# The normalised activations in DRAM by row and channel instead of by channel and row

## The chip, the cores and the metric

The kernel runs on one core of a Trainium2 chip. The core has a matrix engine (TensorE, PE in the profile), three engines for elementwise work (VectorE = DVE, ScalarE = ACT, GpSimd = POOL), a queue engine (SyncE = SP), and 16 DMA engines that move data between DRAM and the on-chip memory of 128 partitions. The metric is the device time of one execution in microseconds. The kernel before takes 7,697.9 us (median of 3, from 7,692.57 to 7,713.86).

## What is computed

The input x has the shape [16, 16, 256, 256] (batch, channel, row, column), in fp32. Two layers follow each other, each with a group norm ahead of it and a residual sum after it:

```python
x = x + L0(_gn(x))       # Fourier layer: FFT, products with poles and residues, back
x = x + L1(_gn(x))       # the layer that the change concerns
```

With the norm's result z in place of x, layer 1 is, cut to its core:

```python
xs = z.reshape(B * C, 1, H, W)
f = mish(conv2d(xs, W1, b1))                    # conv1: 1 -> 4 features, 3x3
top, bot = f[:, :, :H2], f[:, :, H2:]           # upper and lower half of the rows
ker = conv2d(relu(conv2d(bot, Wred, bred)), Wspan, bspan)
top_inv = (patches3x3(top) * ker[:, None]).sum(axis=2)          # involution
shuffled = concatenate([top_inv, roll(bot, -1, axis=1)], 3)     # channels regrouped
out = mish(conv2d(shuffled, W2, b2))            # conv2: 64 -> 16 channels, 3x3
gate = sigmoid(weighted sum of neighbouring channels' means of out)
return z * gate
```

## The kernel before

Four stages run one after the other: `layer0_forward`, `layer0_mix`, `layer0_back` and `layer1`. The tensor zn in DRAM, [16, 16, 258, 258], joins the last two. It holds the norm's result with a border of zeros, so that a 3x3 window needs no special cases.

`layer0_back` (line 753) goes over 16 batches and four groups of four channels. It computes layer 0's result by matmuls (lines 813 and 816), takes the statistics, and writes the norm's result into one of three tiles `zb` (line 830: one half of the channels on VectorE, the other on GpSimd). Two DMAs (line 839) store the tile, each 128 rows of four channels, 1,032 bytes in one piece.

`layer1` (line 849) works by units. A batch has nine: eight with 30 new rows of eight channels (four row blocks j, two channel halves h), and a tail unit with the last rows of all 16 channels. What a unit does:

- `load_rows` (line 913) brings z for the lower half and for the upper half of the picture, in a pool of four buffers. Partition 32 dx + r holds row r of 32, shifted by dx columns, so that the three column taps of the 3x3 filter lie on partitions. Three DMAs bring 32 rows of eight channels each (line 920), two more bring rows 32 and 33 for all three dx (line 928). The tail takes twelve DMAs of ten rows of four channels (line 934). All are issued by SyncE.
- `conv1` (line 940) multiplies 102 partitions (120 in the tail) with the weights. It works by column parity q: one matmul for the odd columns, one for the even ones, each of four channels by 128 columns, and so reads every second column. An fp32 matmul is two passes in the profile.
- `lower` (line 959) applies Mish to the lower half in one activation per group of four channels. `reduce` makes the involution's kernel from it and stores the lower half into the DRAM tensor cf (line 1067, GpSimd's queue).
- `upper` (line 986) does conv1 for the upper half, with eight activations of 32 partitions per group (line 995). `spread` (line 1002) copies them to the shifted partitions on GpSimd. `involution` (line 1010) is one matmul per feature and group and three VectorE operations, and `store_top` writes cf.

Conv2 runs one batch behind. `conv2_rows` (line 1072) loads 17 row pairs from cf on SyncE's queue, in two buffers, and `conv2` (line 1077) makes 48 passes on quarter tiles per call and an activation with a sum. When a batch is done, `gate` (line 1101) reloads z from zn in four parts (line 1113), multiplies by the gate plus the norm's scale (line 1135) and stores the output (line 1136).

The order on TensorE, ScalarE, VectorE and GpSimd is written by hand in the loop at the end of `layer1`. In each step, unit i+2 is loaded, unit i+1 goes through `lower`, `reduce`, `upper` and `spread`, unit i through `involution`, and a piece of conv2 of the batch before is put between them. SyncE carries out its loads in the order in which they are issued. PSUM has two buffers for conv1, three for the involution and reduce, and one for conv2.

Of the kernel before, what the change touches and what calls it, by code (L numbers as in the profile page):

```python
# [18 lines left out]
C = 16  # L19
# [732 lines left out]
@with_exitstack  # L752
def layer0_back(ctx, tc, d, hd, bd, zn, mr, ed):


    nc = tc.nc
    nb = d["x"].shape[0]
    cp = ctx.enter_context(tc.tile_pool(name="bc", bufs=1))
    iy = load(nc, cp, d["iy"], [P, 2, N], "iy")
    ones = load(nc, cp, d["ones"], [P, P], "ones")  # L760

    e1 = cp.tile([P, C, N], F32, name="e1")
    e2 = cp.tile([P, C, N], F32, name="e2")
    for k in range(0, C, 4):
        for i, t in enumerate((e1, e2)):
            nc.sync.dma_start(out=t[:, k : k + 4], in_=ed[:, i, k : k + 4])

    hp = ctx.enter_context(tc.tile_pool(name="bh", bufs=3))
    fp = ctx.enter_context(tc.tile_pool(name="bf", bufs=3))
    sm = ctx.enter_context(tc.tile_pool(name="bs", bufs=2))  # L770
    psf = ctx.enter_context(tc.tile_pool(name="psf", bufs=2, space=PSUM))
    psy = ctx.enter_context(tc.tile_pool(name="psy", bufs=3, space=PSUM))
    psn = ctx.enter_context(tc.tile_pool(name="psn", bufs=1, space=PSUM))

    zero = cp.tile([P, 4, N + 2], F32, name="zero")
    nc.gpsimd.memset(zero, 0.0)
    planes = zn.rearrange("b (p c) y x -> p (b c) y x", p=1)[0]
    for h in range(2):
        for y in (0, N + 1):
            nc.gpsimd.dma_start(out=planes[P * h : P * h + P, y], in_=zero[:, 0])  # L780
    zbuf = [cp.tile([P, 4, 2, N + 2], F32, name=f"zb{i}") for i in range(3)]
    for t in zbuf:
        for x in (0, N + 1):
            nc.gpsimd.memset(t[:, :, :, x : x + 1], 0.0)

    for b in range(nb):
        r2 = fp.tile([P, P], F32, tag="r2", name="r2")
        nc.sync.dma_start(out=r2, in_=bd[b])
        for k0 in range(0, C, 4):
            h = hp.tile([P, 4, 2, N], F32, tag="h", name="h")  # L790
            nc.sync.dma_start(
                out=h.rearrange("p k v x -> p k (v x)"),
                in_=hd[:, b, k0 : k0 + 4].rearrange("f k v x -> f k (v x)"),
            )
            x = hp.tile([P, 4, 2, N], F32, tag="x", name="x")
            nc.sync.dma_start(
                out=x.rearrange("p k h x -> p (k h) x"),
                in_=d["x"][b, k0 : k0 + 4].rearrange("k (h p) x -> p (k h) x", p=P),
            )
            st = sm.tile([P, 4, 6], F32, tag="st", name="st")  # L800
            for k in range(4):
                if k % 2 == 0:
                    pf = psf.tile([P, 2, N], F32, tag="pf", name="pf")
                    nc.tensor.matmul(
                        pf, lhsT=r2, rhs=e1[:, k0 + k : k0 + k + 2], start=True, stop=True
                    )
                    f = fp.tile([P, 2, N], F32, tag="f", name="f")
                    nc.scalar.copy(f, pf)
                py = psy.tile([P, 2, N], F32, tag="py", name="py")
                for yh in range(2):  # L810
                    ys = slice(P * yh, P * yh + P)
# [12 lines left out]
            g0 = k0 // 2  # L824
            nm, rs = mr[:, b, g0 : g0 + 2, 0], mr[:, b, g0 : g0 + 2, 1]
            for _ in group_norm_scalars(nc, sm, psn, ones, mv, 2, nm, rs):
                pass
            z = zbuf[(4 * b + g0 // 2) % 3]
            for g, eng in ((0, nc.vector), (1, nc.gpsimd)):
                eng.tensor_scalar(  # L830
                    z[:, 2 * g : 2 * g + 2, :, 1 : N + 1],
                    x[:, 2 * g : 2 * g + 2],
                    nm[:, g : g + 1],
                    rs[:, g : g + 1],
                    ALU.add,
                    ALU.mult,
                )
            for h in range(2):
                nc.sync.dma_start(
                    out=zn[b, k0 : k0 + 4, 1 + P * h : 1 + P * h + P].rearrange("k p x -> p k x"),  # L840
                    in_=z[:, :, h],
                )


# [4 lines left out]
def layer1(ctx, tc, d, zn, cf, mr, nb):  # L849
# [62 lines left out]

    def load_rows(b, half, j, h):

        z = zp.tile([P, 8, N], F32, tag="z", name="z")
        if j < 4:
            y = H * half + 30 * j
            src = zn[b, 8 * h : 8 * h + 8]
            for dx in range(3):
                nc.sync.dma_start(  # L920
                    out=z[32 * dx : 32 * dx + 32],
                    in_=src[:, y : y + 32, dx : dx + N].rearrange("c y x -> y c x"),
                )
            for i in range(2):

                row = src[:, y + 32 + i, 0:N]
                win = bass.AP(row.tensor, row.offset, [[1, 3], *row.ap])
                nc.sync.dma_start(out=z[96 + 3 * i : 99 + 3 * i], in_=win)
            return z
        y = H * half + 120  # L930
        for dx in range(3):
            for c in range(4):
                p = 40 * dx + 10 * c
                nc.sync.dma_start(
                    out=z[p : p + 10, :4],
                    in_=zn[b, 4 * c : 4 * c + 4, y : y + 10, dx : dx + N].rearrange("c y x -> y c x"),
                )
        return z

    def conv1(z, half, tail, g):  # L940

        k, w = (120, w1t[half]) if tail else (102, w1[half])
        ps = ps1.tile([P, 2, 4, H], F32, tag="c1", name="c1")
        cols = z[:k, 4 * g : 4 * g + 4].rearrange("k c (x q) -> k q c x", q=2)
        for q in range(2):
            nc.tensor.matmul(ps[:, q], lhsT=w, rhs=cols[:, 1 - q], start=True, stop=True)  # L946
        return ps

    class Unit:

# [8 lines left out]
        def lower(self):  # L959

            self.bot = fp.tile([P, 8, 2, H], F32, tag="bot", name="bot")
            for g, cs in enumerate(self.groups):
                ps = conv1(self.z[0], 1, self.tail, g)
                nc.scalar.activation(
                    self.bot[:, cs].rearrange("p c q x -> p q c x"), ps, AF.Mish, bias=b1[1]
                )

        def reduce(self):

# [16 lines left out]
        def upper(self, g):  # L986
# [6 lines left out]
            for f in range(4):  # L993
                for q in range(2):
                    nc.scalar.activation(  # L995
                        self.feat[64 - 32 * q : 96 - 32 * q, f, self.groups[g], :H],
                        ps[32 * f : 32 * f + 32, q],
                        AF.Mish,
                        bias=b1[0][32 * f : 32 * f + 32],
                    )  # L1000
# [100 lines left out]
    def gate(b, acc):  # L1101
# [4 lines left out]
        dst = d["out"][b].rearrange("c (q y) x -> (c q) y x", q=8)  # L1106

        def part(k):
            o = op.tile([P, 8, N + 2], F32, tag="o", name="o")
            src = zn[b, :, 1 + 8 * k, 0:1]  # L1110
            row = N + 2
            src = bass.AP(src.tensor, src.offset, [[row * row, C], [32 * row, 8], [1, 8 * row]])
            nc.sync.dma_start(out=o.rearrange("p y x -> p (y x)"), in_=src)
            return o[:, :, 1 : N + 1]

        o = part(0)
        yield
# [15 lines left out]
        for k in range(4):  # L1133
            following = part(k + 1) if k < 3 else None
            nc.gpsimd.tensor_scalar(o, o, scale, mean2[:, b : b + 1], ALU.mult, ALU.add)  # L1135
            nc.gpsimd.dma_start(out=dst[:, 8 * k : 8 * k + 8], in_=o)
            o = following
            yield

# [67 lines left out]
def layer1_arrays(W1, b1, Wred, bred, Wspan, bspan, W2, b2, Weca):  # L1207
# [43 lines left out]
    g2 = np.repeat(g1[:C], 8, axis=0)  # L1251
    pm = np.zeros((8, C, 3, C, 8), np.float32)
    for k in range(3):
        for c in range(C):
            if 0 <= c + k - 1 < C:
                pm[:, c + k - 1, k, c, :] = 1.0
    return {
        "w1_0": w1.reshape(102, P),
        "w1_1": w1.transpose(0, 2, 1).reshape(102, P),
# [3 lines left out]
        "dw": dw.reshape(P, P),  # L1263
        "dwt": dwt.reshape(P, P),
        "c2": c2.reshape(P, 2, 3, 32),
        "g2": g2,
# [96 lines left out]
def forward(ctx, tc, d):  # L1363
# [43 lines left out]
```

## Time and profile before

| stage | from, us | to, us | what fills it |
|---|---|---|---|
| layer0_forward, layer0_mix | 0 | about 3,050 | not touched by the change |
| layer0_back | about 3,055 | about 3,902 | first load 3,054.7, last store of zn 3,901.6 |
| layer1 | 3,902.3 | 7,700.4 | first load of z to the end |

Busy time over the whole span of 7,700.4 us: TensorE 7,126.0 us (93%), VectorE 4,921.2 (64%), ScalarE 3,678.6 (48%), GpSimd 2,804.5 (36%). The mean granted TensorE clock is 0.965 of full speed. DMA moved 1,442.20 MB, 875.87 MB read from DRAM and 556.47 MB written to it.

Groups that the change touches, with the mean time of one:

| line, engine | what | count | mean ns |
|---|---|---|---|
| L946 PE | conv1 pass, 102 partitions, 512 columns | 2,048 | 646 |
| L946 PE | conv1 pass in the tail, 120 partitions | 128 | 613 |
| L964 ACT | Mish of the lower half, 1,024 elements | 272 | 1,115 |
| L995 ACT | Mish of the upper half, 32 partitions, 512 elements | 2,176 | 680 |
| L830 DVE, POOL | the norm's result into zb, 1,024 elements | 64 each | 812, 1,752 |
| L1135 POOL | gate times z, 2,048 elements | 64 | 2,055 |

How to read them: the means of matmuls contain the overlap of successive passes, so the distance between the weight loads of two passes tells the real pace. A view by slices shows which stage is busy with what; the chain of waits shows what the end of the program hung on; and the waits show who stood still for whom. Idle time of an engine that isn't on the chain costs nothing.

### The profile page before, as it was taken

Reading aid. Unit: us, or ns where it says so; the run is one execution under the profiler, and the core shown is the slowest. Engines: PE = TensorE matmul, PEld = TensorE weight load, DVE = VectorE, ACT = ScalarE, POOL = GpSimd, SP = SyncE. Lnnn points to the kernel's source line nnn. Section 1 sums busy time; section 2 is a strip of 40 time slices with the busy share of each in tenths; the row PEclk is TensorE's granted clock in tenths of the full one; section 3 lists DMA queues with packets and bytes.
Section 4 is the critical chain, followed back from the end, with each engine's and each line's share of the span. In section 5 each row is a group of like instructions: output and inputs, shape, how many; then the busy total and the mean of one; then the engine's idle time right before and its main releaser. Section 6 shows DMA issues by size and latency. Waiting matters only on the chain. (4 is left out here: it accounts for less than half of the span.)

```text
span 7700.4 us, 147483 instructions
## 1 busy us (share of the span) xinstructions
PE 7126.0 (93%) x58728; PEld 4107.7 (53%) x58728; DVE 4921.2 (64%) x9184; ACT 3678.6 (48%) x5387; POOL 2804.5 (36%) x3616
## 2 busy tenths in 40 slices
PE   7889999688888988999978999999999999999997
PEld 5778888566666766777733333333333333333332
DVE  8999865366666665666656666666666666666662
ACT  2223333355555554111146656666566655656662
POOL 2334444200000000111135545555554555555552
PEclk9999999899999999999989999999999999999998
DMA  3444444333333333877757788898888898888896
GB/s 99 112 116 121 120 115 108 111 94 94 94 94 94 92 90 121 261 246 245 246 153 216 217 245 248 260 263 251 249 241 251 249 263 256 248 243 251 246 267 205
DMA packets 936290, 1442.20 MB, mean 187 GB/s; under 512 B 91866, under 2 KB 807958, under 8 KB 903606
## 3 DMA queue, kind: packets, MB, share of 16 engines
q1 hardware_dynamic: 792374, 958.51, 44.6%
q0 software_dynamic: 143232, 474.25, 19.4%
q8 instruction: 469, 7.68, 0.4%
q14 instruction: 215, 1.76, 0.1%
HBM read 875.87 MB, written 556.47 MB: 186 GB/s over the span
## 5 line engine op out<-in xcount | busy, mean ns | idle before, releaser
L995 ACT ACTIVATE wide<-c,b 32x512 f32<-32x512 f32 x2176 | 1479.5, 680 | 372.0 <-PE c L946 319.7
L1023 DVE TENSOR_TENSOR t<-pd,r 64x512 f32<-64x512 f32 x1088 | 744.4, 684 | 1321.8 <-PE pd L1015 1298.9
L1026 DVE TENSOR_TENSOR top<-pd,t 32x512 f32<-32x512 f32 x2176 | 1504.3, 691 | 54.8 <-DMA cf<-top 2.3
L1089 PE MATMUL c2ps<-rows,c 128*32 128x512 f32 x12288 | 1393.4, 600 | 20.6 <-ACT e L1098 14.7
L946 PE MATMUL c<-z,w 102*128 102x512 f32 x2048 | 1053.6, 646 | 140.1 <-ACT wide L995 116.3
L1007 POOL COPY wide<-wide 32x1031 f32<-32x1031 f32 (+1 forms) x576 | 570.1, 990 | 1390.1 <-ACT wide L995 1362.7
L1015 PE MATMUL pd<-wide,dw 128*128 128x512 f32 x2048 | 1012.7, 617 | 6.0 <-ACT r L983 3.2
L1089 PEld LDWEIGHTS c2ps<-rows,c 128*32 128x32 f32 x12288 | 388.7, 109 | 992.3 <-issue 885.1
L946 PEld LDWEIGHTS c<-z,w 102*128 102x128 f32 x2048 | 399.2, 197 | 703.8 <-issue 515.3
L1015 PEld LDWEIGHTS pd<-wide,dw 128*128 128x128 f32 x2048 | 376.7, 194 | 626.5 <-issue 458.2
L692 POOL DMA_DIRECT2D hd<-h x254 | 151.9, 598 | 1373.2 <-DVE h L688 1353.2
L631 DVE COPY s<-ps 128x512 f32<-128x512 f32 x264 | 271.4, 1028 | 508.5 <-PE ps L623 487.2
L1008 POOL COPY wide<-wide 32x1031 f32<-32x1031 f32 (+1 forms) x576 | 573.4, 996 | 35.9
L1098 ACT ACTIVATE e<-c2ps,b 128x512 f32<-128x512 f32 x256 | 176.0, 687 | 855.3 <-PE c2ps L1089 852.7
L313 PE MATMUL px<-wxn,u 128*64 128x256 f32 x4224 | 558.7, 385 | 2.1 <-ACT o L320 1.8
L813 PE MATMUL py<-h,iy 128*128 128x256 f32 x2048 | 541.5, 383 | 5.2 <-issue 5.2
L623 PE MATMUL ps<-tt,lt 128*64 128x256 f32 x4224 | 496.1, 385 | 37.9 <-DVE lt L609 37.3
L642 PE MATMUL pg<-alb,s 128*32 128x64 f32 x16896 | 310.6, 240 | 196.3 <-issue 185.2
L675 PE MATMUL ph<-ix,yt 64*128 64x256 f32 x4128 | 480.4, 382 | 0.7 <-ACT yt L662 0.7
L313 PEld LDWEIGHTS px<-wxn,u 128*64 128x64 f32 x4224 | 401.1, 136 | 127.4 <-ACT o L320 5.3
L813 PEld LDWEIGHTS py<-h,iy 128*128 128x128 f32 x2048 | 385.2, 191 | 108.4 <-issue 50.0
L675 PEld LDWEIGHTS ph<-ix,yt 64*128 64x128 f32 x4128 | 389.0, 187 | 89.9 <-issue 49.2
(202 smaller groups left out, 10343.7 us busy)
## 6 DMA issues: line engine op xcount, KB each, us to landing
rows<-cf SPq DMA_DIRECT2D x128, 2176.0 KB
z<-zn SPq DMA_DIRECT2D x768, 256.0 KB
cf<-top POOLq DMA_DIRECT2D x512, 240.0 KB, 7.3
cf<-bot POOLq DMA_DIRECT2D x96, 840.0 KB, 10.4
alc<-al SPq DMA_DIRECT2D x264, 256.0 KB
zn<-zb SPq DMA_DIRECT2D x128, 516.0 KB
o<-zn SPq DMA_DIRECT2D x64, 1032.0 KB
z<-in_x SPq DMA_DIRECT2D x64, 1024.0 KB
```

Source lines behind the costliest of these rows:

```text
L313: nc.tensor.matmul(ps[64 * k : 64 * k + 64, :, h], lhsT=u[:, h, part, g0 + j + k].rearrange("p f c -> p (f c)"), rhs=wxn[:, h, part], star ...
L623: nc.tensor.matmul(ps[64 * h : 64 * h + 64, v], lhsT=lt[:, h, k, 1 - v : 3 - v].rearrange("p l f c -> p (l f c)"), rhs=tt[:, h, k], start= ...
L675: nc.tensor.matmul(ph[q][:, e], lhsT=yt[lanes, i].rearrange("p t k -> p (t k)"), rhs=ix[lanes, i], start=n == 0, stop=n == 3,)
L813: nc.tensor.matmul(py[:, yh], lhsT=iy[:, v, ys], rhs=h[:, k, v], start=v == 0, stop=False)
L946: nc.tensor.matmul(ps[:, q], lhsT=w, rhs=cols[:, 1 - q], start=True, stop=True)
L995: nc.scalar.activation(self.feat[64 - 32 * q : 96 - 32 * q, f, self.groups[g], :H], ps[32 * f : 32 * f + 32, q], AF.Mish, bias=b1[0][32 * ...
L1007: nc.gpsimd.tensor_copy(flat[0:32, f, 1:m], flat[64:96, f, 0 : m - 1])
L1008: nc.gpsimd.tensor_copy(flat[96:128, f, 0 : m - 1], flat[32:64, f, 1:m])
L1015: nc.tensor.matmul(ps, lhsT=dwt if self.tail else dw, rhs=self.feat[:, f, cs, :H], start=True, stop=True,)
L1023: nc.vector.tensor_tensor(t[64:128], ps[:64], self.r[:, cs], ALU.mult)
L1026: nc.vector.tensor_tensor(self.top[32 * f : 32 * f + 32, cs, q], ps[lanes], t[lanes], ALU.add)
L1089: nc.tensor.matmul(ps[32 * j : 32 * j + 32], lhsT=c2[:, blk, dx, :], rhs=t[:, 4 * j + blk : 4 * j + blk + 4, x : x + H], start=(blk, dx) = ...
```

## The change

zn becomes [16, 258, 16, 258]: batch, padded row, channel, padded column. The eight channels that a unit takes of one row now lie in one piece of DRAM, 8 x 1,032 bytes. This is meant to replace many short pieces by few long ones, and to let conv1 read contiguous columns:

- `layer0_back` writes its tile in the order half, channel, column, and each DMA stores 4,128 bytes in one piece. The zero borders take two DMAs from 16 partitions in place of four from 128.
- `load_rows` makes one DMA of 96 pieces of 8,248 bytes (the last two columns are left out, since dx shifts the start by up to two), one of six pieces, and in the tail three of 40 pieces of 4,120 bytes.
- `conv1` takes two channels by 256 contiguous columns per matmul. The parities are separated where ScalarE reads PSUM, with a stride of two. `lower` therefore makes two activations per group, one for each parity.
- `gate` loads each part by eight DMAs of 16 partitions in pieces of 1,024 bytes, with partitions in the order (piece of rows, channel) instead of (channel, piece of rows). The output's DMA and the constants `pm` and `g2` follow that order.

```diff
-    zero = cp.tile([P, 4, N + 2], F32, name="zero")
+    zero = cp.tile([nb, C * (N + 2)], F32, name="zero")
     nc.gpsimd.memset(zero, 0.0)
-    planes = zn.rearrange("b (p c) y x -> p (b c) y x", p=1)[0]
-    for h in range(2):
-        for y in (0, N + 1):
-            nc.gpsimd.dma_start(out=planes[P * h : P * h + P, y], in_=zero[:, 0])
-    zbuf = [cp.tile([P, 4, 2, N + 2], F32, name=f"zb{i}") for i in range(3)]
+    for y in (0, N + 1):
+        nc.gpsimd.dma_start(out=zn[:, y].rearrange("b c x -> b (c x)"), in_=zero)
+    zbuf = [cp.tile([P, 2, 4, N + 2], F32, name=f"zb{i}") for i in range(3)]
...
-                    z[:, 2 * g : 2 * g + 2, :, 1 : N + 1],
-                    x[:, 2 * g : 2 * g + 2],
+                    z[:, :, 2 * g : 2 * g + 2, 1 : N + 1],
+                    x[:, 2 * g : 2 * g + 2].rearrange("p k h x -> p h k x"),
...
-                    out=zn[b, k0 : k0 + 4, 1 + P * h : 1 + P * h + P].rearrange("k p x -> p k x"),
-                    in_=z[:, :, h],
+                    out=zn[b, 1 + P * h : 1 + P * h + P, k0 : k0 + 4].rearrange("p k x -> p (k x)"),
+                    in_=z[:, h].rearrange("p k x -> p (k x)"),
...
-        z = zp.tile([P, 8, N], F32, tag="z", name="z")
+        z = zp.tile([P, 8, N + 2], F32, tag="z", name="z")
+        flat = z.rearrange("p c x -> p (c x)")
+        row = C * (N + 2)
         if j < 4:
-            y = H * half + 30 * j
-            src = zn[b, 8 * h : 8 * h + 8]
-            for dx in range(3):
-                nc.sync.dma_start(
-                    out=z[32 * dx : 32 * dx + 32],
-                    in_=src[:, y : y + 32, dx : dx + N].rearrange("c y x -> y c x"),
-                )
-            for i in range(2):
-
-                row = src[:, y + 32 + i, 0:N]
-                win = bass.AP(row.tensor, row.offset, [[1, 3], *row.ap])
-                nc.sync.dma_start(out=z[96 + 3 * i : 99 + 3 * i], in_=win)
+
+            m = 8 * (N + 2) - 2
+            src = zn[b, H * half + 30 * j, 8 * h, 0:1]
+            win = bass.AP(src.tensor, src.offset, [[1, 3], [row, 32], [1, m]])
+            nc.sync.dma_start(out=flat[:96, :m], in_=win)
+            win = bass.AP(src.tensor, src.offset + 32 * row, [[row, 2], [1, 3], [1, m]])
+            nc.sync.dma_start(out=flat[96:102, :m], in_=win)
             return z
-        y = H * half + 120
+        m = 4 * (N + 2) - 2
+        src = zn[b, H * half + 120, 0, 0:1]
         for dx in range(3):
-            for c in range(4):
-                p = 40 * dx + 10 * c
-                nc.sync.dma_start(
-                    out=z[p : p + 10, :4],
-                    in_=zn[b, 4 * c : 4 * c + 4, y : y + 10, dx : dx + N].rearrange("c y x -> y c x"),
-                )
+            win = bass.AP(src.tensor, src.offset + dx, [[4 * (N + 2), 4], [row, 10], [1, m]])
+            nc.sync.dma_start(out=flat[40 * dx : 40 * dx + 40, :m], in_=win)
         return z

     def conv1(z, half, tail, g):

         k, w = (120, w1t[half]) if tail else (102, w1[half])
-        ps = ps1.tile([P, 2, 4, H], F32, tag="c1", name="c1")
-        cols = z[:k, 4 * g : 4 * g + 4].rearrange("k c (x q) -> k q c x", q=2)
-        for q in range(2):
-            nc.tensor.matmul(ps[:, q], lhsT=w, rhs=cols[:, 1 - q], start=True, stop=True)
-        return ps
+        ps = ps1.tile([P, 2, 2, N], F32, tag="c1", name="c1")
+        for a in range(2):
+            c = 4 * g + 2 * a
+            nc.tensor.matmul(ps[:, a], lhsT=w, rhs=z[:k, c : c + 2, 0:N], start=True, stop=True)
+        return [ps.rearrange("p a c (x e) -> p (a c) e x", e=2)[:, :, 1 - q] for q in range(2)]
...
-                nc.scalar.activation(
-                    self.bot[:, cs].rearrange("p c q x -> p q c x"), ps, AF.Mish, bias=b1[1]
-                )
+                for q in range(2):
+                    nc.scalar.activation(self.bot[:, cs, q], ps[q], AF.Mish, bias=b1[1])
...
-            o = op.tile([P, 8, N + 2], F32, tag="o", name="o")
-            src = zn[b, :, 1 + 8 * k, 0:1]
-            row = N + 2
-            src = bass.AP(src.tensor, src.offset, [[row * row, C], [32 * row, 8], [1, 8 * row]])
-            nc.sync.dma_start(out=o.rearrange("p y x -> p (y x)"), in_=src)
-            return o[:, :, 1 : N + 1]
+            o = op.tile([P, 8, N], F32, tag="o", name="o")
+            for q in range(8):
+                y = 1 + 32 * q + 8 * k
+                nc.sync.dma_start(
+                    out=o[C * q : C * q + C],
+                    in_=zn[b, y : y + 8, :, 1 : N + 1].rearrange("y c x -> c y x"),
+                )
+            return o
...
-            nc.gpsimd.dma_start(out=dst[:, 8 * k : 8 * k + 8], in_=o)
+            m = 8 * N
+            nc.gpsimd.dma_start(
+                out=dst[:, :, m * k : m * k + m], in_=o.rearrange("p y x -> p (y x)")
+            )
...
-    zn = dram.tile([nb, C, N + 2, N + 2], F32, name="zn")
+    zn = dram.tile([nb, N + 2, C, N + 2], F32, name="zn")
```

More of the change, by code (lines that the diff above doesn't have):

```diff
@@ L996, in upper @@
                         self.feat[64 - 32 * q : 96 - 32 * q, f, self.groups[g], :H],
-                        ps[32 * f : 32 * f + 32, q],
+                        ps[q][32 * f : 32 * f + 32],
                         AF.Mish,
@@ L1105, in gate @@
         nc.vector.tensor_reduce(total, acc, AX.X, ALU.add)
-        dst = d["out"][b].rearrange("c (q y) x -> (c q) y x", q=8)
+        dst = d["out"][b].rearrange("c (q y) x -> q c (y x)", q=8)
         def part(k):
-            o = op.tile([P, 8, N + 2], F32, tag="o", name="o")
-            src = zn[b, :, 1 + 8 * k, 0:1]
-            row = N + 2
-            src = bass.AP(src.tensor, src.offset, [[row * row, C], [32 * row, 8], [1, 8 * row]])
-            nc.sync.dma_start(out=o.rearrange("p y x -> p (y x)"), in_=src)
-            return o[:, :, 1 : N + 1]
+            o = op.tile([P, 8, N], F32, tag="o", name="o")
[6 more added lines that the diff above has]
+            return o
         o = part(0)
@@ L1250, in layer1_arrays @@
     g1 = np.tile((cs[:, None] // 2 == np.arange(G)).astype(np.float32), (8, 1))
[L1251 to L1252 removed]
+    pm = np.zeros((8, C, 3, 8, C), np.float32)
     for k in range(3):
@@ L1255, in layer1_arrays @@
             if 0 <= c + k - 1 < C:
-                pm[:, c + k - 1, k, c, :] = 1.0
+                pm[:, c + k - 1, k, :, c] = 1.0
     return {
@@ L1265, in layer1_arrays @@
         "c2": c2.reshape(P, 2, 3, 32),
-        "g2": g2,
+        "g2": g1,
         "pm": pm.reshape(P, 3, P),
```

## The prediction

> **What bounds the kernel now.** I read the slices first, to find the stages, and then the chain of waits.
>
> ```profile
> PE   7889999688888988999978999999999999999997
> PEclk9999999899999999999989999999999999999998
> DMA  3444444333333333877757788898888898888896
> PE 43%; ACT 2%; issue 1%; DMA 1%; POOL 0%; DVE 0%; POOLq 0%; ACTq 0%; SPq 0%; DVEq 0%
> PE c2ps L1089 17%; PE c L946 12%; PE pd L1015 12%; PE pr L974 2%; ACT wide L995 2%; DMA o<-zn 0%; DMA out_dram<-o 0%; ACT L995 0%; PE pg L1120 0%; DVE top L1026 0%; POOL o L1135 0%; DMA cf<-top 0%; POOL wide L1008 0%; ACT e L1098 0%; POOL wide L1007 0%
> ```
>
> The chain covers layer 1 (from 3902 us to the end) and is TensorE nearly throughout: conv2, conv1 and the involution. So layer 1 is matmul-bound. The busy time by stretch agrees, both there and in the stage that writes zn:
>
> ```profile
> core 0: us, PE busy (x) PEld busy (x) DVE busy (x) ACT busy (x) POOL busy (x), PEclk, DMA share, GB/s
> 3450.00:3650.00 200.00, 199.50 (x866) 156.56 (x864) 123.12 (x320) 21.18 (x46) 26.36 (x15) 1.00 0.79 246
> 4500.00:5000.00 500.00, 486.48 (x2443) 172.86 (x2443) 310.01 (x461) 299.99 (x446) 262.40 (x334) 0.98 0.87 251
> ```
>
> layer0_back has TensorE at 99.7% and layer 1 at 97%. But layer 1 also keeps the DMA engines at 0.87. In it conv1 waits for ScalarE only 26 times in 3000 us, and for loads not at all:
>
> ```profile
> PE c L946 <- ACT wide L995: 74.3, 26, 3.5
> ```
>
> The weight loads give each matmul's pace, since one starts per pass:
>
> ```profile
> 5138.16 0.19 PEld L946 LDWEIGHTS c<-z,w 102*128 102x128 f32 x1 [0.26 <-issue]
> 5138.61 0.19 PEld L946 LDWEIGHTS c<-z,w 102*128 102x128 f32 x1 [0.26 <-issue]
> 5139.94 0.19 PEld L1015 LDWEIGHTS pd<-wide,dw 128*128 128x128 f32 x1 [0.24 <-PE c L946]
> 5140.37 0.19 PEld L1015 LDWEIGHTS pd<-wide,dw 128*128 128x128 f32 x1 [0.24 <-issue]
> ```
>
> Conv1, on every second column, takes 0.4515 us per pass (seven intervals, 5135.90 to 5139.06). The involution, on contiguous columns, takes 0.4335. That is all that the contiguous columns can win: 18 ns.
>
> One more view decides the forecast, the DMA issues:
>
> ```profile
> z<-zn SPq DMA_DIRECT2D x768, 256.0 KB
> cf<-top POOLq DMA_DIRECT2D x512, 240.0 KB, 7.3
> alc<-al SPq DMA_DIRECT2D x264, 256.0 KB
> ```
>
> SyncE's loads have no time to landing: this view gives one only where every DMA of a semaphore shows 16 completion events, and here they don't. The next part uses that.
>
> [...] Its eight SyncE semaphores hold 32,390 events. [...] alc<-al is the instructive one. Its source counts [8][8] rows of 4,096 B, its destination 64 partitions, so k=8. In the packet records of the trace, 7 to 9 of its packets are in flight from 1889.25 to 1892 us, though two such copies are queued. So both use the same eight engines. Loads from 128 partitions show 16 in flight.
>
> [...] The trace shows 4% lost; the measurement decides. [...] the copy that reads PSUM at stride 64 (L649) takes 586 ns, as contiguous ones do (L445, 585).
>
> **The change part by part.**
> *Conv1 columns.* 2,048 + 128 passes by 18 ns: 39 us less TensorE time, if TensorE still bounds.
> *Activations.* `lower` splits one of 1,024 elements (1,115 ns) into two of 512. At 685 each (L995 680, L1098 687), that is +0.255 us for each of 272 groups: 69 us of ScalarE. In a full unit conv2 (5.4 us) lies between them and their reader. In the tail step nothing does, so at most 0.5 us for each of 16 batches: 8 us.
> *layer0_back.* Rows of 1,032 B become 4,128 B; VectorE and GpSimd write the same elements in another order. If VectorE's 812 ns became 1.5 times as long, that is 0.4 us in a 13 us step in which it is 62% busy. TensorE's 99.7% hides it. The larger memset (16,512 B a partition, about 4 us by L907's 3.5 us for as many) lies before GpSimd's first use.
> *Loads and stores of the gate.* 1,024-byte rows instead of 8,256. In the tail of the trace the first move at 350 GB/s, the second at 230. Off the path except at the very end: -5 us. The output's destination now counts [8][16], so k=8; it took 10.3 us of a 26 us step with 16, and nothing waits but a later store.
> The permuted constants (`pm`, `g2`) cost nothing: same sizes, loaded once. SyncE issues 2,037 copies instead of 2,645, at about 0.45 us each; it is not the bound.
> *Loads for conv1: here it goes wrong.* The new window is [[1,3],[row,32],[1,m]] into 96 partitions: slowest dimensions 3 and 96, so k=3. 792 KB per load goes through three engines, always the same. The two further rows have [2][3] against 6: k=2. The tail has [4][10] against 40: k=4. Formerly the rows loads had 32 against 32: k=16.
>
> **The busiest engine, per batch of eight units and a tail.** The price of a row of 8,248 B is bounded by two rows of the packet records. h<-hd, 8,192 B: 311 ns. o<-zn, 8,256 B from the same zn: with nothing beside it (7607 to 7620 us) 580 to 620 ns each, 16 in flight, 230 GB/s; 312 only for first packets or between store packets. I take 595, since 8,248 B lies above 8,192 and has the same source. Each unit then: 2 x 32 x 0.595 = 38.1; the two rows 2 x 3 x 0.595 = 3.6; conv2's rows, 2,176/16 = 136 packets of 1,024 B at 48.5 ns (46 to 51 when saturated) = 6.6. Eight units: 386. The tail: 60 packets of 4,120 B at 0.16 (4,096 B: 159 ns) = 9.6. The gate: 256 packets at 48.5 ns = 12.4. Sum 408 us. The stores (about 5 us a unit) I count as nothing: they fit the pauses of the long rows, since from 7537 to 7544 us o<-zn kept its 23 to 28 packets per us with 8,192-byte stores between them.
>
> Now a batch takes 228.5 us (the chain's conv2 pieces at 6628.10 and 7085.18 lie two batches apart). So the loads take TensorE's place as the bound, and its 39 us and ScalarE's 69 us disappear in waiting. Four z buffers let the queue run one unit ahead, so that the engines have work all the time.
>
> What is queued behind: SyncE's queue is in order, so conv2's rows stand behind z on the slow engines; TensorE, ScalarE, VectorE and the stores then wait for z.
>
> Total: layer 1 before is 3,779 us from its first matmul (3921.7), of which 15 x 228.5 = 3,427 are full batches and about 148 and 203 the first (no conv2) and last (no conv1). After: start 3,932; first batch 8 x 41.7 + 10 = 344; 15 x 408 = 6,120; last 195. Sum 10,591, so **10,600 us**.
>
> **Rivals.**
> *Fast rows* (15%): the long rows move at 0.314 with no pauses. For: h<-hd, and first packets. Against: 13 us of steady 600 ns. Then the stores add their 5 us: 8 x (70 x 0.314 + 6.6 + 5.0) + 22 + 12 = 302 a batch: 3,932 + 230 + 4,530 + 195 = 8,890 us.
> *All 16 engines after all* (10%): the split follows the 96 partitions. Against: alc has this very form and shows eight. TensorE stays the bound: 7,698 - 39 + 8 - 5 = 7,662 us, faster.
> *Spread, but the gain is eaten* by ScalarE in the tail steps or the split stores (3%): within 0.3%, about 7,700.
> *Stores not hidden* (10%): 408 + 8 x 5 + 12 = 460 a batch: 11,400 us.
> *Main case*: 62%, with 0.57 to 0.61 a row giving 10,350 to 10,800.
>
> **How the numbers follow.** Slower is the main case, fast rows and unhidden stores: 0.87; faster 0.10; same 0.03. The range runs from below fast rows (8,800) to 11,300; it leaves out the 16-engine cases and most of the unhidden stores, some 2 in 10.
>
> **What would show it.** Right: conv1 waiting for z<-zn for thousands of us; three packets of 8,248 B in flight, near 595 ns; GB/s in layer 1 near half of 250; conv1's passes at 0.434; bot's activations twice as many at 685; 23,270 events on SyncE's semaphores[...]. Wrong: 16 long rows in flight, and TensorE still 97% busy; or rows at 314.

## The result, and the profile after

The changed kernel takes 9,621.5 us (median of 4, from 9,596.3 to 9,629.4) against 7,698.3 us beside it: ratio 1.249, 95% interval 1.246 to 1.252. The forecast was 10,600, with a range from 8,800 to 11,300. A batch of layer 1, from one gate to the next, takes 357 us (mean of the third to the thirteenth; the fourteen full ones run from 338 to 363) in place of 228.7.

The slices and the chain of waits of the kernel after:

```profile
PE   7899988888888999677667757657766766766766
PEclk9999999999999999888888878878878878878888
DMA  3444442333334776355666665655656566566566
...
PE 39%; DMA 34%; SPq 6%; issue 3%; POOL 1%; ACT 1%; another core or an unknown queue 1%; DVE 0%; POOLq 0%; ACTq 0%; DVEq 0%
DMA rows<-cf 20%; DMA z<-zn 9%; PE c2ps L1080 7%; PE ps L623 5%; PE py L811 5%; PE ph L675 4%; DMA o<-zn 4%; PE c L938 4%; PE pd L1006 4%; PE pg L642 3%; SPq L921 3%; PE py L814 2%; SPq L923 2%; PE pt L658 1%; PE pf L802 1%
```

Each slice is 240 us here, and layer 1 fills them from the seventeenth on. In it TensorE is at 5 to 7 tenths, and the DMA engines fall too, from 8 or 9 tenths before to mostly 5 or 6. That fits an uneven load: the mean over 16 engines would say "half idle" while a few of them set the time. The chain now runs over transfers, and most over conv2's rows, whose own loads the change leaves as they were. The stretches say the same:

```profile
core 0: us, PE busy (x) PEld busy (x) DVE busy (x) ACT busy (x) POOL busy (x), PEclk, DMA share, GB/s
3450.00:3650.00 200.00, 199.47 (x867) 156.36 (x865) 123.85 (x324) 21.23 (x46) 26.34 (x15) 1.00 0.71 249
4500.00:5000.00 500.00, 331.73 (x1534) 116.45 (x1534) 195.35 (x289) 194.70 (x308) 181.07 (x230) 0.82 0.61 162
```

layer0_back kept its 99.7%: the new order of its elements is hidden, as forecast. In layer 1 every engine lost about a third of its busy time, and the bytes moved per second fell from 251 to 162 GB/s. From 4500 to 7500 us TensorE waits for these:

```profile
PE c2ps L1080 <- DMA rows<-cf: 715.9, 51, 32.0
...
PE c L938 <- DMA z<-zn: 278.7, 39, 19.8
```

In the kernel before, the same stretch has next to nothing of either, and what it has stands at conv1's weight loads:

```profile
PEld c L946 <- DMA z<-zn: 0.7, 3, 0.2
PEld c L946 <- DMA rows<-cf: 0.5, 2, 0.2
```

What the change was to bring is there as well. The weight loads of conv1 (L938) now come every 0.43 us, like the involution's (L1006), and the lower half's activations, in the page's groups (busy, mean ns of one), take 684 ns each:

```profile
6506.70 0.19 PEld L938 LDWEIGHTS c<-z,w 102*128 102x128 f32 x1 [0.24 <-issue]
6507.13 0.19 PEld L938 LDWEIGHTS c<-z,w 102*128 102x128 f32 x1 [0.24 <-issue]
6508.42 0.19 PEld L1006 LDWEIGHTS pd<-wide,dw 128*128 128x128 f32 x1 [0.24 <-issue]
6508.85 0.19 PEld L1006 LDWEIGHTS pd<-wide,dw 128*128 128x128 f32 x1 [0.24 <-issue]
```

```profile
L957 ACT ACTIVATE bot<-c,b 128x512 f32<-128x512 f32 x544 | 344.5, 684 | 552.7 <-issue 333.7
```

The DMA issues show one z load where there were three, and again no time to landing:

```profile
z<-zn SPq DMA_DIRECT2D x256, 773.2 KB
```

The split over engines has to be read from two places that no table prints. The first is SyncE's eight completion semaphores, the counters that tell when a copy is done. They hold 2,888 + 2,942 + 2,945 + 2,874 + 2,862 + 2,939 + 2,926 + 2,894 = 23,270 events, the forecast number exactly. Every copy of one kind leaves the same number there. In the kernel before it is 16 for the z loads of 32 rows, 4 for a window of three columns (3 pieces of the source's slowest dimension against 3 partitions), 11 for a tail load (10 against 10) and 9 for alc (8 against 64); with the 16 of nearly all the others, its 2,645 copies make up the 32,390. In the kernel after it is 4 for a load of long rows (3 against 96), 3 for the two further rows (2 against 6), 5 for a tail load (4 against 40) and 16 for each of the gate's. Where it is below 16, one event comes some 0.2 to 0.4 us after SyncE has issued the copy (median 0.42 for the long rows) and the others later, the second after another 21.8 us (median) there. The k of the recorded texts is the number without that early event (the "closing event" of the expectation for `swapped`). The second place is the packet records: each has the start, the duration and the size of one piece moved, but not the engine. Some long row (8,248 B) is in flight for 4,040 us of the run, and more than three are for only 74 us of that; some row of the tail (4,120 B) for 362 us, and more than four for 4. From 4500 to 9000 us the median of a long row is 314 ns and the mean 378.

### The profile page after: what moved, and what is told of

Same layout as the page of the kernel before. It is cut to its first block, busy times and chain, and to the rows that moved or that the text cites. A ratio compares the mean times of both kernels' runs of the same rounds, so it can differ in the third digit from the quotient of the medians.

```text
span 9620.4 us, 146903 instructions
## 1 busy us (share of the span) xinstructions
PE 7345.8 (76%) x58728; PEld 4184.1 (43%) x58728; DVE 4921.9 (51%) x9184; ACT 3721.4 (39%) x5659; POOL 2789.2 (29%) x3614
## 4 chain that ended last, share of the span: by engine, by line
PE 39%; DMA 34%; SPq 6%; issue 3%; POOL 1%; ACT 1%; another core or an unknown queue 1%; DVE 0%; POOLq 0%; ACTq 0%; DVEq 0%
DMA rows<-cf 20%; DMA z<-zn 9%; PE c2ps L1080 7%; PE ps L623 5%; PE py L811 5%; PE ph L675 4%; DMA o<-zn 4%; PE c L938 4%; PE pd L1006 4%; PE pg L642 3%; SPq L921 3%; PE py L814 2%; SPq L923 2%; PE pt L658 1%; PE pf L802 1%
## 5 line engine op out<-in xcount | busy, mean ns | idle before, releaser
L1080 PE MATMUL c2ps<-rows,c 128*32 128x512 f32 x12288 | 1571.6, 664 | 1293.7 <-DMA rows<-cf 1279.9
L938 PE MATMUL c<-z,w 102*128 102x512 f32 x2048 | 1084.5, 667 | 556.0 <-DMA z<-zn 544.1
L1080 PEld LDWEIGHTS c2ps<-rows,c 128*32 128x32 f32 x12288 | 438.1, 119 | 2396.6 <-issue 2359.4
L1006 PE MATMUL pd<-wide,dw 128*128 128x512 f32 x2048 | 996.9, 608 | 12.5 <-POOL wide L999 7.0
L938 PEld LDWEIGHTS c<-z,w 102*128 102x128 f32 x2048 | 429.3, 214 | 1148.3 <-issue 1066.2
L1006 PEld LDWEIGHTS pd<-wide,dw 128*128 128x128 f32 x2048 | 369.4, 191 | 612.6 <-issue 438.3
L957 ACT ACTIVATE bot<-c,b 128x512 f32<-128x512 f32 x544 | 344.5, 684 | 552.7 <-issue 333.7
L207 PE MATMUL pu<-fy,eo 128*128 128x128 f32 x2048 | 425.3, 291 | 11.7 <-DVE u L224 7.5
```

Of the source, the lines that this page charges most:

```text
L938: nc.tensor.matmul(ps[:, a], lhsT=w, rhs=z[:k, c : c + 2, 0:N], start=True, stop=True)
L1006: nc.tensor.matmul(ps, lhsT=dwt if self.tail else dw, rhs=self.feat[:, f, cs, :H], start=True, stop=True,)
L1080: nc.tensor.matmul(ps[32 * j : 32 * j + 32], lhsT=c2[:, blk, dx, :], rhs=t[:, 4 * j + blk : 4 * j + blk + 4, x : x + H], start=(blk, dx) = ...
```

## The experiments

**Is it the split, or the new layout?** `swapped` changes the order in which one copy counts its pieces, and nothing else in the loads; the weights' rows follow.

```diff
-            win = bass.AP(src.tensor, src.offset, [[1, 3], [row, 32], [1, m]])
+            win = bass.AP(src.tensor, src.offset, [[row, 32], [1, 3], [1, m]])
...
-                k = 32 * dx + i if i < 32 else 96 + 3 * (i - 32) + dx
+                k = 3 * i + dx
```

> Theory (the split over three DMA engines): the same 96 pieces of 8,248 B in the same one DMA, only counted rows first (32) and columns second (3)[...]; the rows of the conv1 weights follow that order. 12 packets of the big load per engine instead of 32 on three. TensorE is the bound again: 7,698 - 39 (conv1 passes) + 8 (tail activations) - 5 (gate) = about 7,660 us, ratio 0.993 to 1.00, 16 long rows in flight. SyncE's semaphores: 23,270 + 256 x 13 (16 events in place of 3) - 256 (no closing event) = 26,342. Rival (long pieces, or the new layout itself, are slow): nothing but the order of two dimensions has changed, so the time stays near 9,620 us, or at least over 9,000.

Measured: 7,747.9 us, ratio 1.0059 [1.0046, 1.0072], and 26,342 events, exactly: 12 more for each of the 256 loads of long rows. Sixteen and more long rows are now in flight at a time. So 1,874 of the 1,923 us that the change cost come from the order of two dimensions. But it is not the 7,660 that I expected. Something keeps 88 us, and the trace of `swapped` says who waits (4500 to 7500 us):

```profile
PE c2ps L1080 <- DMA rows<-cf: 40.1, 13, 8.9
```

A batch takes 230.5 us on average, and the end from the last gate 41 us.

`old_k3` is the opposite test: the kernel before, with its old layout and its pieces of 1,024 B, loaded in windows that count 3 against 96, as those of the long rows do, of which three were in flight in the kernel after.

```diff
-            for dx in range(3):
-                nc.sync.dma_start(
-                    out=z[32 * dx : 32 * dx + 32],
-                    in_=src[:, y : y + 32, dx : dx + N].rearrange("c y x -> y c x"),
-                )
+            for c in range(8):
+                first = src[c, y : y + 32, 0:N]
+                win = bass.AP(first.tensor, first.offset, [[1, 3], *first.ap])
+                nc.sync.dma_start(out=z[:96, c], in_=win)
```

> The kernel before with its old layout and its pieces of 1,024 B, but the 32-row loads as eight windows [[1,3],[row,32],[1,256]] per load (k=3) in place of three loads with k=16. Theory (three engines are the cause): per unit 2 x 272 packets x 48 ns = 26 us on each of three engines, rows of conv2 6.6, stores 5: 38 us x 8 plus tail and gate 21 = 322 us a batch if the engines never pause, 380 if they pause as in the changed kernel (357 measured against 302 worked out): 9,200 to 10,100 us. Rival (the long pieces are the cause): pieces are short here, so TensorE stays the bound and the time stays near 7,700.

Measured: 9,242.9 us, ratio 1.200 [1.198, 1.202]; a batch takes 330 us, near the 322 of the sum. Short pieces on three engines are slow too, though less so (330 us a batch against 357). So the length of the pieces is not the cause. The stretch from 4500 to 5000 us has the same signature as after:

```profile
4500.00:5000.00 500.00, 343.75 (x1642) 117.12 (x1642) 200.96 (x298) 196.45 (x293) 175.61 (x224) 0.83 0.55 171
```

`dose4` counts the long rows 4 against 32. The tail's loads, 4 against 40, had four rows in flight in the kernel after, so four engines are taken for the long rows too.

```diff
-            win = bass.AP(src.tensor, src.offset, [[1, 3], [row, 32], [1, m]])
-            nc.sync.dma_start(out=flat[:96, :m], in_=win)
+            for dx in range(3):
+                win = bass.AP(src.tensor, src.offset + dx, [[row, 4], [4 * row, 8], [1, m]])
+                nc.sync.dma_start(out=flat[32 * dx : 32 * dx + 32, :m], in_=win)
```

> The changed kernel with each 32-row load as three DMAs, by column, counted [[row,4],[4 row,8]] so that k=4; the rows come in another order than the weights have them, so conv1 multiplies other rows. Theory (time goes with the share of the busiest engine): 48 long pieces a unit on each of four engines x 0.314 = 15.1, two rows 1.9, conv2's rows 6.6, stores 5: 28.6 us x 8 + gate and tail 32 = 261 us a batch when the engines never pause, 308 with the ratio 357/302 measured with three engines: 8,240 to 8,950 us. Rival (any split below 16 is equally bad, or three DMAs in place of one change nothing): near 9,620; rival (four engines are enough): near 7,750.

Measured: 8,902.8 us, ratio 1.155 [1.153, 1.157]; 311 us a batch. Three engines, four, sixteen: 357, 311, 230 us. The time went with the share of the busiest engine until TensorE was the bound, and it lies some 50 us over the sum of the packets with four engines as with three.

**What are the contiguous columns worth?** `old_cols` takes only the changed conv1 and its activations into the kernel before.

```diff
-        ps = ps1.tile([P, 2, 4, H], F32, tag="c1", name="c1")
-        cols = z[:k, 4 * g : 4 * g + 4].rearrange("k c (x q) -> k q c x", q=2)
-        for q in range(2):
-            nc.tensor.matmul(ps[:, q], lhsT=w, rhs=cols[:, 1 - q], start=True, stop=True)
-        return ps
+        ps = ps1.tile([P, 2, 2, N], F32, tag="c1", name="c1")
+        for a in range(2):
+            c = 4 * g + 2 * a
+            nc.tensor.matmul(ps[:, a], lhsT=w, rhs=z[:k, c : c + 2, 0:N], start=True, stop=True)
```

> The kernel before, old layout and old loads, with conv1 on contiguous columns and the parities separated by ScalarE (twice as many activations in the lower half). Theory: 2,176 passes x 18 ns = 39 us saved, up to 8 us lost in the tail steps: 7,659 to 7,667 us, ratio about 0.995. Rival (the split activations, or PSUM reads at a stride of two, are what costs): 7,700 us or more, with conv1 waiting for ScalarE.

Measured: 7,666.2 us, ratio 0.9958 [0.9945, 0.9970], 31.5 us less. TensorE's busy time fell by 33.8 us (7,126.0 to 7,092.2), ScalarE's rose by 37 (3,678.6 to 3,715.9), hidden.

**What keeps the 88 us of `swapped`?** `out16`, built on `swapped`, orders the gate's partitions by channel and piece, as the kernel before does. With that its store of the output counts 128 rows against 128 partitions. (The constants `pm` and `g2` follow; their lines are left out here.)

```diff
-                    out=o[C * q : C * q + C],
+                    out=o[q:P:8],
...
-        dst = d["out"][b].rearrange("c (q y) x -> q c (y x)", q=8)
+        dst = d["out"][b].rearrange("c (q y) x -> (c q) (y x)", q=8)
...
-                out=dst[:, :, m * k : m * k + m], in_=o.rearrange("p y x -> p (y x)")
+                out=dst[:, m * k : m * k + m], in_=o.rearrange("p y x -> p (y x)")
```

> The kernel of the run swapped (big loads over 16 engines, 7,748 us), with the gate's partitions ordered by channel and piece as in the kernel before, so that the output's store counts 128 rows and 128 partitions (k=16) in place of [8][16] (k=8). swapped took 231 us a batch where contiguous columns alone took 226, and 41 us from the last gate to the end in place of 29. Theory (the store over half of the engines holds up the queues): batches back to 226 to 228 us and 10 us less at the end: 7,670 to 7,700 us, ratio about 0.998. Rival (the gate's 32 small loads on SyncE's in-order queue, in place of four, hold up conv2's rows): unchanged, within 0.2% of 7,748.

Measured: 7,651.7 us, ratio 0.9933 [0.9920, 0.9945]: 96 us less than `swapped` and faster than both kernels. Batches are at 226.1 us, and the end from the last gate at 29. The stretch is back where it was before the change:

```profile
4500.00:5000.00 500.00, 487.60 (x2491) 175.76 (x2490) 316.26 (x470) 312.01 (x494) 261.90 (x338) 0.98 0.82 250
```

The store's time from issue to landing, in `swapped` and in `out16`:

```profile
out_dram<-o POOLq DMA_DIRECT2D x64, 1024.0 KB, 13.9
out_dram<-o POOLq DMA_DIRECT2D x64, 1024.0 KB, 9.0
```

The last store of the run has the queues to itself. Its 128 packets of 8,192 B go with 8 in flight and take 7.3 us in `swapped`; in `out16` they go with 16 in flight and take 2.7. So the store does use twice the engines. Two things change with it: the partitions that the gate's loads write to, and 128 packets of 4 B that each store of `swapped` carries beyond those of `out16`. The store's k is therefore the likeliest cause of the 96 us and not the only one possible. The 32 small loads are not it: they are all still there.

`out16_tail`, built on `out16`, also splits the tail's loads, from 4 against 40 (five events a copy in the kernel after) to 10 against 10 (eleven in the kernel before): k=4 to k=10.

```diff
-            win = bass.AP(src.tensor, src.offset + dx, [[4 * (N + 2), 4], [row, 10], [1, m]])
-            nc.sync.dma_start(out=flat[40 * dx : 40 * dx + 40, :m], in_=win)
+            for c in range(4):
+                p = 40 * dx + 10 * c
+                win = bass.AP(src.tensor, src.offset + dx + 4 * (N + 2) * c, [[row, 10], [1, m]])
+                nc.sync.dma_start(out=flat[p : p + 10, :m], in_=win)
```

> out16 with the tail's three loads (k=4, 60 pieces per engine and batch of 161 ns, 9.7 us on four engines) split by channel into twelve of ten rows (k=10, 24 pieces). Theory: the tail's loads lie off the path, TensorE being the bound: within 0.2% of out16. Rival (the last uneven loads still delay conv2's rows behind them): 10 to 30 us less than out16. Nothing but the two-row loads (k=2) is then left of the uneven splits.

Measured: 7,658.0 us, ratio 0.9941 [0.9927, 0.9954]. No gain, as expected of loads that nothing waits for.

**Why 357 us a batch, and not the 302 of my rival "fast rows"?** `few_stores` leaves the stores to cf out from batch 4 on.

```diff
-            store_bot(self.b, self.j, self.h, self.bot)
+            if self.b < 4:
+                store_bot(self.b, self.j, self.h, self.bot)
...
-                store_top(self.b, self.j, self.h, self.top)
+                if self.b < 4:
+                    store_top(self.b, self.j, self.h, self.top)
```

> The changed kernel with the stores of both halves to cf left out from batch 4 on (conv2 then reads the older contents of cf); everything else runs. The sum gave a batch 302 us with 40 us of stores in it; 357 was measured. If the three engines are simply always busy with more than I counted: 357 - 40 = about 317 us a batch. If the missing 55 us come from stores and long rows sharing an engine: 262 to 275. If stores fit the pauses, as the prediction had it: 350 to 357.

Measured: 9,094.4 us (one run); from batch 4 on a batch takes 314 us, 43 less. So the stores cost about what they were priced at in the rival's sum (40), and they were not hidden. The missing 55 us are elsewhere.

From one start of conv2 to the next, the steps of the kernel after (means of 13 batches) point at the gate:

```
step                        0     1     2     3     4     5     6    7 and tail
kernel before, us          26.1  26.0  26.1  26.0  26.1  26.0  24.3  48.0
kernel after, us           54.2  54.4  49.9  33.7  39.7  35.4  26.8  61.0
```

Steps 3 to 5, at 36 us on average, are near the 33.6 us that the rival counted for a unit; steps 0 to 2, with the gate's loads, are 16 us longer: some 50 us in all, nearly the missing 55. SyncE's own timeline there:

```profile
6296.76 47.91 SPq L1103 DMA_DIRECT2D o<-zn  x8
6346.20 0.71 SPq L921 DMA_DIRECT2D z<-zn  x1
6348.75 0.61 SPq L923 DMA_DIRECT2D z<-zn  x1
6349.46 0.70 SPq L921 DMA_DIRECT2D z<-zn  x1
```

For 48 us SyncE stands in the eight loads of one part; the next z loads come after, and from 6332 to 6348 us no long row begins. From 6290 to 6410 us SyncE's longest wait is for the gate's product on GpSimd, which frees the tile:

```profile
SPq L1103 <- POOL o L1128: 53.8, 2, 32.3
```

Four runs each take away something that could hold it up. `rows_act` issues conv2's rows from ScalarE, `k3_gate_pool` the gate's loads from GpSimd, `k3_gate_one` makes one load of eight, and `k3_out16` is the edit of `out16` on the changed kernel.

```diff
-        nc.sync.dma_start(out=t[:, :, 1 : N + 1], in_=flat[:, 16 * s : 16 * s + 17])
+        nc.scalar.dma_start(out=t[:, :, 1 : N + 1], in_=flat[:, 16 * s : 16 * s + 17])
```

> The changed kernel with conv2's row loads issued from ScalarE's queue instead of SyncE's; the z loads keep their three engines. Theory (in-order issue: SyncE stands about 29 us in one z load[...], and conv2's rows behind it are issued late): with the rows out of that queue the engines stay fed and a batch falls from 357 towards the 302 us of the sum: 8,800 to 9,100 us. Rival (the pauses come from the engines themselves, or from the z buffers coming free late): within 1% of 9,620 us.

```diff
-                nc.sync.dma_start(
+                nc.gpsimd.dma_start(
                     out=o[C * q : C * q + C],
```

> The changed kernel (big loads on three engines, 9,621 us) with the gate's 32 loads a batch issued from GpSimd's queue instead of SyncE's. In the changed kernel the steps without a gate take 34 to 40 us and the three with it 50 to 54, and SyncE stands 32 to 48 us in each part's loads. Theory (the gate's loads wait in SyncE's in-order queue for a free tile and for the completion of earlier copies, and the next z loads stand behind them, so that the three engines run dry): the three steps fall to about 40, a batch from 357 to 305 to 320 us, 8,850 to 9,050 us in all. Rival (the gate's packets themselves take that time on the three engines): unchanged, 9,550 to 9,650.

```diff
-            for q in range(8):
-                y = 1 + 32 * q + 8 * k
-                nc.sync.dma_start(
-                    out=o[C * q : C * q + C],
-                    in_=zn[b, y : y + 8, :, 1 : N + 1].rearrange("y c x -> c y x"),
-                )
+            src = zn[b, 1 + 64 * k, 0, 0:1]
+            src = bass.AP(src.tensor, src.offset, [[8 * (N + 2), P], [1, 8 * N]])
+            nc.sync.dma_start(out=o.rearrange("p y x -> p (y x)"), in_=src)
```

> The changed kernel with each part of the gate loaded by one copy of 128 pieces of 8,192 B in place of eight copies of 16 partitions; the bytes are as many, but not the right ones, so the gate multiplies other values. Theory A (SyncE's eight completion semaphores, used in turn, make each of the 32 copies wait for the eighth before it): a batch falls to 305 to 330 us, 8,850 to 9,250 in all. Theory B (the first copy of each part waits for a free tile, however many copies follow): a batch stays within 10 us of 357.

> The changed kernel with the gate's partitions by channel and piece, as in the run out16, so that the output's store has k=16; the z loads keep three engines. It was worth 96 us with the loads on 16 engines. Theory B (the tile comes free late because its store takes long on eight engines): the gate's steps shorten, a batch falls by 10 to 40 us, 9,000 to 9,450 us. Rival (the store is not what the tile waits for): within 1% of 9,621.

```
run            us        ratio to before          us a batch
rows_act       9,645.2   1.253 [1.251, 1.255]     352
k3_gate_pool   9,532.3   1.237 [1.235, 1.240]     348
k3_gate_one    9,405.0   1.220 [1.218, 1.222]     340
k3_out16       9,527.5   1.236 [1.234, 1.238]     352
```

None was worth more than 17 us of 357. What `rows_act` gains in the later batches it loses before the first gate, which comes 51 us later. In it the waits have changed places: from 4500 to 7500 us conv1 waits 10 us for z in place of 279, conv2 982 us for its rows in place of 716, and ScalarE, which now issues them, has 281 us of waits for z. In `k3_gate_pool` the three steps became 38.8, 63.6 and 33.1 us: the hold-up moved. (From GpSimd's queue the gate's pieces also move as packets of 4,096 B instead of 1,024: in `k3_z_alone`, which issues them so too, a run has 65,536 packets under 2 KB fewer than the changed kernel, 517,494 against 583,030.) SyncE then stood in the z loads instead:

```profile
6312.35 45.20 SPq L921 DMA_DIRECT2D z<-zn  x1
```

So the theory that one thing queued ahead of z costs the 55 us fell, for each of the three. The last run puts z alone on SyncE's queue, with six tiles. (Six tiles with nothing else changed were not tried.)

```diff
-    zp = ctx.enter_context(tc.tile_pool(name="l1z", bufs=4))
+    zp = ctx.enter_context(tc.tile_pool(name="l1z", bufs=6))
...
-        nc.sync.dma_start(out=t[:, :, 1 : N + 1], in_=flat[:, 16 * s : 16 * s + 17])
+        nc.scalar.dma_start(out=t[:, :, 1 : N + 1], in_=flat[:, 16 * s : 16 * s + 17])
...
-                nc.sync.dma_start(
+                nc.gpsimd.dma_start(
```

> The changed kernel with its three-engine z loads alone on SyncE's queue (conv2's rows on ScalarE's, the gate's loads on GpSimd's) and six z tiles in place of four. Taken one at a time, moving the rows gave 5 us a batch, moving the gate's loads 9, one gate load per part 17, the output over 16 engines 6; 302 was worked out and 357 measured. If the missing 55 us are pauses in which nothing is queued for the three engines (the sum of the small obstacles): a batch near 302 to 315 us, 8,800 to 9,000 us in all. If the three engines have work and take longer over it than the sum of their packets (long rows, short rows and stores that share an engine): above 335 us, 9,300 us or more.

Measured: 10,492.0 us, ratio 1.362 [1.359, 1.364], a batch 413 us: slower than the changed kernel. The number falls under the second case (above 335 us), but the trace doesn't show what that case supposed, engines that always have work. The waits from 4500 to 7500 us and SyncE's timeline:

```profile
PE c2ps L1080 <- DMA rows<-cf: 1268.2, 29, 60.1
```

```profile
6342.69 0.60 SPq L923 DMA_DIRECT2D z<-zn  x1
6411.71 0.69 SPq L921 DMA_DIRECT2D z<-zn  x1
```

Conv2's rows now come up to 60 us late, and meanwhile no z is issued for 68 us. The packet records suggest why. From 6332 to 6348 us 11 to 15 long rows and 10 to 15 short ones begin in each 2 us, in step with each other, as if an engine took one packet from each of its queues in turn. That is my reading of the equal counts; the records don't name the engine. If so, a row of conv2 waits for a long row on those three engines, 136 times in a load (2,176 rows over 16 engines). TensorE stands before conv2, and SyncE waits for conv1 to free a z tile: 2,257 us from 4500 to 9000. The three engines run dry after all: for 53 us of a batch no packet of 8,248 or 1,024 B, no store and no load of the gate is in flight. Which of the three moves did the harm was not separated. `rows_act`, with the rows alone on another queue, took about as long as the changed kernel.

## Why the prediction was right, and where its sum was not

*The engines.* The forecast took each copy's number of engines from how its two sides count. The sums gave 23,270 events after and 26,342 for `swapped`; both came out to the last one. Three long rows are in flight after, sixteen in `swapped`. That holds for the copies of this case; a rule for any counts was not shown. The direction of the forecast rests on this alone, and `swapped`, `old_k3` and `dose4` show it from three sides.

*Conv1, activations, layer0_back.* 0.43 us a pass, 684 ns an activation, 99.7%: all as forecast. By themselves the columns bring 31.5 us; 39 less up to 8 had been worked out.

*"I take 595, since 8,248 B lies above 8,192 and has the same source."* Wrong, and the largest error. "Rows at 314" was one of the prediction's own signs of being wrong, and that is the median where three engines move them. The 595 had been measured on rows of zn with 16 in flight. The mean is 378, and more than half of what lies above 314 comes from company: rows with eight or more packets of 1,024 B in flight, and no store, take 531 ns (mean; 266 rows a batch). The prediction's sum has 560 long rows on the busiest engine in a batch, so 595 in place of 378 is 122 us too many.

*"The stores I count as nothing."* Wrong the other way: `few_stores` gives 43 us a batch. On the three engines that set the pace they did not fit into pauses.

*"So that the engines have work all the time."* 408 - 122 + 43 = 329; measured 357, and what makes up the other 28 stays open. Pauses in the long rows are seen, as from 6332 to 6348 us while SyncE stood in the gate's loads. But the measure that gave 53 us of empty time a batch in `k3_z_alone` gives 1.4 us here, and since the records don't name the engine, pauses of the three engines alone can't be read. Taken one at a time, the rows' place in the queue, the gate's loads and its store are worth 5 to 17 us a batch, and in `k3_z_alone`, which moves two of them together, a batch grew longer. The rival "fast rows" had the bare row right and would have needed this rest to be nothing: 302 a batch, 8,890 us.

*"Conv1 waiting for z<-zn for thousands of us."* The wait lies elsewhere. Over the whole run conv1 waits 544 us for z and conv2 1,280 for its rows, which stand behind z in SyncE's queue (issued at 6296.28 us, say, behind four z loads from 6292.48), as the prediction had said. The rate fell to 162 GB/s and not near half of 250, since the loads took less time than forecast.

*The total.* 9,621 lies in neither case, but between "fast rows" (8,890) and the main case (10,350 to 10,800). The range took in both. A row priced too high was set off in part by stores and a rest priced at nothing, so the sum came 10% too high where the rows alone would have put it further off. That is luck; the mechanism, three engines in place of sixteen, is not.

*The gate: "k=8 ... nothing waits but a later store."* The store lands 13.9 us after its issue instead of 10.3, and the edit that gives it 16 engines is worth 94 us beside the three engines (`k3_out16`) and 96 once TensorE is the bound again (`out16`). With `out16` the case "all 16 engines", 7,662 us, is met at 7,651.7; with the store as the change has it, it would have missed by 86.

## What to carry to other kernels

Look at how both sides of a copy count. Here a window with the three column shifts outermost had three of its rows in flight (9,621 us), and the same window with two dimensions swapped had sixteen (7,748 us). The DMA engines' mean busy share, 0.61 from 4500 to 5000 us in the kernel after, did not tell this; the packets in flight of one size, and the completion events on the semaphores, did. And when a few engines become the bound, count everything that they carry: the stores, taken as hidden in the forecast, gave 43 us a batch when they were left out.

## What the runs showed of the hardware that was not expected

The price of a row of zn went with how many engines move such rows. A row of 8,248 B takes 314 ns (median) where three engines do, and 487 in `out16`, where sixteen do. This isn't so for every row: in the kernel before, the 8,192-byte rows of h<-hd take 311 with 15 to 17 of them in flight. What tells the two apart was not tested.

TensorE was also slower after a wait. In the kernel after, conv2's 48 passes take 5.44 us (median of 148 calls) with no wait ahead of them, and 7.57 (median of 70 calls, 6.7 to 8.3) after waits of more than 6 us. The granted clock from 4500 to 5000 us is 0.82, against 0.98 before. One call of each kind:

```profile
6498.23 5.43 PE L1080 MATMUL c2ps<-rows,c 128*32 128x512 f32 x48
...
6522.43 8.15 PE L1080 MATMUL c2ps<-rows,c 128*32 128x512 f32 x48 [11.70 <-DMA rows<-cf]
```

Long pieces won no time here: once both were spread over 16 engines, contiguous columns on the old layout (0.9958 [0.9945, 0.9970]) and the new layout with 16-way loads and store (0.9933 [0.9920, 0.9945]) lie within a quarter of a per cent of each other, in batches of 226.4 and 226.1 us.
